# Sorted rows that carry their weight, place and batch; results scattered to token and choice; the last residual in four parts

## The chip, the cores and the metric

The kernel runs on one core of a Trainium2 chip. It is written in the Tile framework: the program names tiles and operations, the framework places the tiles, orders each engine's instructions and puts in the waits. The engines are TensorE (PE, with its weight loads shown as PEld), VectorE (DVE), ScalarE (ACT), GpSimd (POOL) and SyncE (SP). Here SP issues all plain transfers and POOL all transfers whose rows are picked by an index. Each engine takes its instructions strictly in order, so an instruction that waits holds everything behind it on that engine.

The metric is the device time of one execution in microseconds. Before the change it is 1390.96 us (median of 3 runs, 1390.5 to 1391.24).

## The reference

One block of a transformer on 2 x 1024 tokens of width 256, all in float32: attention with 16 heads of 128 (one key and value head shared by all), then a mixture of experts, 2 of 8 for each token. Both are modulated by a condition vector. Cut to what matters:

```python
h = layernorm(x) * (1 + ca) + sa
x = x + ga * attention(h)            # ends in a layernorm of its output
h = layernorm(x) * (1 + cb) + sb
x = x + gb * moe(h)

def moe(x):                          # T = 2048 tokens, H = 256, I = 176, E = 8, K = 2
    logits = x @ router_w.T
    vals, idx = top_k(logits, K)
    w = softmax(vals)
    order = argsort(idx.reshape(-1))
    xs = x[order // K]               # rows sorted by expert
    y1 = ragged_dot(xs, w1, counts)
    gate, up = split(y1, 2)
    y2 = ragged_dot(silu(gate) * up, w2, counts)
    return (y2[argsort(order)] * w[:, None]).reshape(T, K, H).sum(1)
```

`gb` is one row of 256 factors for each of the two batches.

## The kernel before

The 2048 tokens are 16 tiles of 128 rows (NT), 8 for each batch. Attention goes over them in 4 blocks of 4 tiles. In a block, for each of 16 heads and 8 key tiles, PE makes scores (L425), ACT takes the exponential (L429), PE multiplies by the values (L440) and DVE adds up the denominators (L445). Other work hangs between these steps, placed by hand through `at(h, j, f, ...)`: the queries of the next block, the settling of the block before. After the heads comes the output projection `project` (L494).

`Settle` takes a block from projection to routing. `residual` (L528 to L540) normalises the projected rows, multiplies them by `gg` and adds them to `xs`, the running activations. `norms` and `logits` (L553, L556) make the modulated, normalised rows, kept in `rows`, and multiply them by the router's matrix. `weights` picks the best two experts of a token and their shares. `count` and `bases` work out the place of each (token, choice) in a list sorted by expert, whose parts are filled up to whole tiles of 128 rows. The sums of the normalisations need `rsqrt` (L175, L176), two small operations on POOL.

There are two sorted lists (`SETS`). Set 0 holds the tokens of the first three blocks (12 tiles, 24 token and choice tiles; 31 sorted tiles with the filling). Set 1 holds those of the last block (4 tiles; 15 sorted tiles). `scatter` (L683) is an indirect DMA on POOL that writes 128 rows of `rows` to their places in `sorted_x`, a DRAM tensor that was filled with zeros earlier (L259). Set 0 is scattered while the last block's heads run, in eight groups of three; set 1 has to wait until the last block is settled.

Then the sorted tiles run, 46 of them, in a software pipeline. In step m of the loop at L922:

- `Sorted(i, m)` issues the load of 128 rows from `sorted_x` on SP (L821), into one of four buffers;
- `turn` transposes tile m on PE (L827) and copies it out of PSUM (L830 on DVE or L832 on ACT, by parity);
- `up` multiplies tile m-1 by its expert's first matrix (L845), whose place is read from a register, then silu on ACT (L853) and the product on DVE (L855);
- `turn_back` transposes tile m-3 (L861) and copies it (L864 or L866);
- `down` multiplies tile m-4 by the second matrix (L879), copies the result (L888 or L890) to `ysb`, and SP writes it to `sorted_y` (L891).

Between these stand the settling of the last block (steps 1 to 8) and, in step 9, its eight scatters. From step NM[0] + 4 = 35 on, each step also gathers for one token tile: two indirect loads on POOL (L898) fetch the rows of the two choices from `sorted_y` by `place_i`. `combine` two steps later takes the first by its share on ACT (L909), adds the second by its share on DVE (L910), multiplies by `gb` (L914), adds `xs` (L915), and SP stores the tile (L916). The gathers of set 0 can only start when all 31 sorted tiles of set 0 are in DRAM, those of set 1 when all 15 of set 1 are.

The framework orders indirect transfers that write the same tensor one after the other: their rows are only known at run time, so it can't tell that they don't overlap.

## Time and profile before

| | |
|---|---|
| median of 3 runs | 1390.96 us |
| the profiled execution, its own time | 1394.08 us |
| its span, first to last instruction | 1392.3 us |
| PE busy in the span | 1334.5 us, 96% |
| DVE, ACT, POOL busy | 681.3, 486.5, 212.2 us |
| projection of the last block ends | 1215.4 us |
| first result tile of the sorted part leaves (L891) | 1237.06 us |
| last scatter of set 1 issued (L683) | 1274.60 us |
| first gather of set 0 (L898) | 1316.67 us |
| last matmul ends | 1371.7 us |
| first gather of set 1 | 1375.46 us |
| last store issued | 1389.1 us |

Times within the profile are counted from the span's start. "Busy" is the time in which an engine worked on an instruction; PE's clock is granted by a throttle, and the profile shows it as a fraction of full speed. In the order of time each line has start and duration in us, engine, source line and operation, the tiles written and read, the shape, how many were merged, and in brackets the idle time just before and what ended it. A line of the waits has the waiting engine and line, the releaser, total us, how often, and the longest. A line of the chain of waits has start, us, and what the end of the kernel was waiting for then.

### The profile page before, as it was taken

The page shows a single profiled execution, that of the slowest core. Times are in us where ns is not written, and L with a number is a line of the kernel's source. Part 1 is how long each engine was busy: PE and PEld are TensorE (multiplying, and loading weights), DVE is VectorE, ACT ScalarE, POOL GpSimd, SP SyncE. Part 2 cuts the span into 40 slices and gives each one's busy share as a digit, 9 for nine tenths or more (in the row PEclk, how much of TensorE's full clock was granted, in tenths as well). Part 3 has the DMA queues.
Part 4 walks back from the last instruction along what each step waited for, and adds up shares of the span by engine and source line. Part 5 has one row for each costly group of instructions (what it writes and reads, how often), then busy time and mean ns, then how long its engine had stood idle before and what let it go on. Part 6 is the DMA issues. An engine that isn't in the chain of part 4 may idle for free.

```text
span 1392.3 us, 12605 instructions
## 1 busy us (share of the span) xinstructions
PE 1334.5 (96%) x4024; PEld 692.9 (50%) x4024; DVE 681.3 (49%) x1378; ACT 486.5 (35%) x947; POOL 212.2 (15%) x303
## 2 busy tenths in 40 slices
PE   7899999999999999999999999999999999989954
PEld 3444444447444444456444444474444444757733
DVE  6356665643636454545464545335474435263343
ACT  2433344441333433322333333313343333133221
POOL 4210312110100010001100000001002230002152
PEclk9999999999999999999999999999999999989977
DMA  7000000000006000010000300000000121114342
GB/s 238 1 1 31 0 31 0 31 0 31 0 0 204 1 30 0 31 31 1 0 32 0 113 0 31 1 31 0 0 31 23 53 87 46 38 57 137 111 144 91
DMA packets 44050, 58.90 MB, mean 42 GB/s; under 512 B 5008, under 2 KB 32656, under 8 KB 43984
## 3 DMA queue, kind: packets, MB, share of 16 engines
q1 hardware_dynamic: 40912, 49.70, 10.9%
q0 software_dynamic: 3072, 8.39, 2.0%
q8 instruction: 33, 0.54, 0.2%
q14 instruction: 33, 0.27, 0.1%
HBM read 39.60 MB, written 18.48 MB: 42 GB/s over the span
## 4 chain that ended last, share of the span: by engine, by line
PE 88%; DMA 4%; DVE 3%; POOL 2%; issue 2%; another core or an unknown queue 0%; ACT 0%; SPq 0%; POOLq 0%; DVEq 0%; ACTq 0%
PE s L425 30%; PE o L440 30%; PE q L388 7%; PE pr L494 7%; PE su L845 3%; PE sy L879 3%; DMA sorted_x<-hT,to 2%; PE qp L402 2%; PE den L454 1%; POOL y L898 1%; PE kv L331 1%; DMA y<-sorted_y,place_i 1%; PE ap L861 1%; PE xp L827 1%; DMA sorted_y<-ysb 1%
## 5 line engine op out<-in xcount | busy, mean ns | idle before, releaser
L425 PE MATMUL s<-qT,kT 128*128 128x512 f32 x1024 | 524.1, 594 | 0.0
L440 PE MATMUL o<-p,vs 128*128 128x512 f32 x1024 | 522.8, 593 | 1.1 <-ACT p L429 1.1
L429 ACT ACTIVATE p<-s 128x512 f32<-128x512 f32 x512 | 305.8, 597 | 502.0 <-PE s L425 491.2
L445 DVE TENSOR_TENSOR sum<-sum,p 128x512 f32<-128x512 f32 x384 | 264.3, 688 | 181.7 <-ACT p L429 177.5
L440 PEld LDWEIGHTS o<-p,vs 128*128 128x128 f32 x1024 | 193.3, 190 | 234.7 <-issue 231.5
L425 PEld LDWEIGHTS s<-qT,kT 128*128 128x128 f32 x1024 | 187.1, 190 | 205.4 <-issue 204.4
L175 POOL TENSOR_SCALAR rn_q<-rn_q 128x4 f32<-128x4 f32 x64 | 15.2, 237 | 722.4 <-DVE rn_q L291 707.3
L388 PE MATMUL q<-wq_sb,hT 128*128 128x512 f32 x256 | 121.9, 599 | 0.0
L494 PE MATMUL pr<-wout_sb,qT 128*128 128x256 f32 x512 | 113.0, 380 | 0.1
L494 PEld LDWEIGHTS pr<-wout_sb,qT 128*128 128x128 f32 x512 | 96.6, 190 | 19.3 <-issue 4.3
L445 DVE TENSOR_TENSOR sum<-p,p 128x512 f32<-128x512 f32 x64 | 44.1, 690 | 111.7 <-ACT p L429 111.5
L291 DVE TENSOR_REDUCE rn_q<-sq_q 128x4 f32<-128x512 f32 x64 | 43.7, 684 | 84.1 <-ACT sq_q L290 84.1
L176 POOL TENSOR_TENSOR rn_q<-rn_q,minus_half 128x4 f32<-128x4 f32 x64 | 82.6, 1291 | 5.3
L388 PEld LDWEIGHTS q<-wq_sb,hT 128*128 128x128 f32 x256 | 49.2, 193 | 60.6 <-issue 50.5
L845 PE MATMUL su<-w_sb,xT 128*128 x184 | 67.5, 491 | 10.6 <-ACT xT L832 5.0
L294 DVE TENSOR_TENSOR vn_q<-q,rn_q 128x512 f32<-128x512 f32 x64 | 44.2, 690 | 58.7 <-POOL rn_q L176 58.7
L290 ACT ACTIVATE sq_q<-q 128x512 f32<-128x512 f32 x64 | 38.2, 597 | 76.0 <-PE q L388 71.6
L462 DVE RECIPROCAL rden<-den 128x512 f32<-128x512 f32 x16 | 53.7, 3357 | 19.3 <-PE den L454 19.3
L470 DVE TENSOR_TENSOR qT<-qT,wide 128x512 f32<-128x512 f32 x64 | 42.3, 688 | 42.5 <-DMA wide<-spread 42.3
L879 PE MATMUL sy<-w2s,sactT 128*128 x184 | 51.4, 406 | 8.5 <-ACT y L909 5.5
L402 PEld LDWEIGHTS qp<-ident,vn_q 128*128 128x128 f32 x256 | 32.2, 143 | 37.3 <-issue 31.5
L447 ACT COPY qT<-o 128x512 f32<-128x512 f32 x64 | 37.5, 586 | 22.7 <-PE o L440 22.7
(155 smaller groups left out, 762.8 us busy)
## 6 DMA issues: line engine op xcount, KB each, us to landing
wide<-spread SPq DMA_DIRECT2D x64, 256.0 KB
x<-sorted_x SPq DMA_DIRECT2D x46, 128.0 KB
sorted_y<-ysb SPq DMA_DIRECT2D x46, 128.0 KB
sorted_x<-zero SPq DMA_DIRECT2D x1, 3968.0 KB
w_sb<-in_w_dram SPq DMA_DIRECT2D x2, 1408.0 KB
wout_sb<-in_wout_dram SPq DMA_DIRECT2D x1, 2048.0 KB
out_dram<-res SPq DMA_DIRECT2D x16, 128.0 KB
sorted_x<-zero SPq DMA_DIRECT2D x1, 1920.0 KB
```

The costliest lines, as they stand in the source:

```text
L176: nc.gpsimd.tensor_tensor(out, out, minus_half[:, : out.shape[1]], ALU.pow)
L294: nc.vector.tensor_tensor(vn, src, rn.unsqueeze(2).to_broadcast([P, n, DH]), ALU.mult)
L388: nc.tensor.matmul(q.rearrange("p h d -> p (h d)"), hT[:, self.blk * QT + i, c, :], wq_sb[:, c, ts(g, QB)], start=(c == 0), stop=(c == DC ...
L402: nc.tensor.transpose(tp[:, j, :], qn[:, j, :], ident)
L425: nc.tensor.matmul(s, kT[:, ts(b * NJ + j, P)], q.head(h), start=True, stop=True)
L429: nc.scalar.activation(p, s, AF.Exp)
L440: nc.tensor.matmul(outs[h], vs[:, b * NJ + j, :], p, start=(j == 0), stop=(j == NJ - 1))
L445: nc.vector.tensor_tensor(sums[h], first, p, ALU.add)
L462: nc.vector.reciprocal(rden, den)
L494: nc.tensor.matmul(ps, q.head(h)[:, ts(i, P)], wout_sb[:, h, :], start=(h == 0), stop=(h == HEADS - 1),)
L845: nc.tensor.matmul(u, self.xT[:, c, :], w1_flat[:, c * I2 :][:, bass.ds(at, I2)], start=(c == 0), stop=(c == DC - 1),)
L879: nc.tensor.matmul(y, self.actT[:, c, :], w2_flat[:, c * D :][:, bass.ds(at, D)], start=(c == 0), stop=(c == 1),)
```

## The change

Each sorted row grows from 256 to 260 words: the choice's weight, the row of the result that it belongs to (token x 2 + choice, an integer), and the batch. The first choice's weight is written where it is made, in `rows`; before the second choices are scattered, POOL copies the second weights and rows over the first (`choose_second`). Empty places of a sorted tile point to rows past the end, filled in with the zeros.

With that, `down` can finish a row by itself: it multiplies by the weight and by the gate of the row's batch in the one operation that takes the result out of PSUM (DVE), and an indirect DMA on POOL writes the rows to `results`, in the order of token and choice. For set 0, which holds tokens of both batches, `gates` makes the gate of each row on DVE. Reading back is then a plain load on SP of 128 x 2 x 256 words (`fetch`), and `combine` is two additions on DVE. ACT makes both PSUM copies `xT` and `sactT` of each tile now, before they went by turns to ACT and DVE.

The loads of sorted tiles are issued up to 7 steps ahead (`PRE`). The first three have buffers of their own; all others share 12 buffers (`RING`) with the fetches, and such a buffer is held until its tile's scatter has read its indices. The fetches of set 0 start in step 38.

The last block's `residual` is split: the statistics right after the projection, then one token tile in each of the steps 0 to 3; norms, logits, weights, count, bases and scatters of that block follow two to three steps later than before, with the scatters right after `bases`. All first choices of a set are scattered before all second ones.

```diff
-    hT = keep.tile([P, NT, DC, P], FP, name="hT")
-    rows = hT.rearrange("p t c q -> p t (c q)")
+    WEIGHT, TO, BATCH, ROW = D, D + 1, D + 2, D + 4
+    rows = keep.tile([P, NT, ROW], FP, name="rows")
+    hT = rows[:, :, :D].rearrange("p t (c q) -> p t c q", q=P)
...
+    for i, (t0, t1) in enumerate(SETS):
+        first_to = rows[:, t0:t1, TO].bitcast(I32)
+        nc.gpsimd.iota(
+            second_to[:, t0:t1], [[TOP * P, t1 - t0]], base=0, channel_multiplier=TOP
+        )
+        nc.vector.tensor_copy(first_to, second_to[:, t0:t1])
+        nc.vector.tensor_scalar(second_to[:, t0:t1], second_to[:, t0:t1], 1, None, ALU.add)
+    for b in range(B):
+        nc.vector.memset(rows[:, b * TPB : (b + 1) * TPB, BATCH:], float(b))
...
-    sorted_y = [dram.tile([n * P, D], FP, name=f"sorted_y{i}") for i, n in enumerate(NM)]
+    results = [
+        dram.tile([(TOP * (t1 - t0) + 1) * P, D], FP, name=f"results{i}")
+        for i, (t0, t1) in enumerate(SETS)
+    ]
...
+        def choose_second(t0, t1):
+            nc.gpsimd.tensor_copy(rows[:, t0:t1, WEIGHT], share[:, t0:t1])
+            nc.gpsimd.tensor_copy(rows[:, t0:t1, TO].bitcast(I32), second_to[:, t0:t1])
...
+        RING = 12
+        PRE = 7
+        FETCH = sum(NM) - 1 - PRE
+        def row_buffer(name):
+            return mg.tile([P, TOP * D], FP, tag="x", name=name, bufs=RING)
...
-                self.x = mx.tile([P, D], FP, tag="x", name=f"x_{self.m}")
+                if self.m < EARLY:
+                    self.x = mx.tile([P, ROW], FP, name=f"x_{self.m}")
+                else:
+                    self.x = row_buffer(f"x_{self.m}")[:, :ROW]
...
-                ysb = mg.tile([P, D], FP, tag="ysb", name=f"ysb_{m}")
-                if m % 2:
-                    nc.scalar.copy(ysb, y)
-                else:
-                    nc.vector.tensor_copy(ysb, y)
-                nc.sync.dma_start(out=sorted_y[self.i][ts(self.at, P), :], in_=ysb)
+                ysb = mg.tile([P, D], FP, tag="ysb", name=f"ysb_{m}", bufs=4)
+                nc.vector.scalar_tensor_tensor(
+                    ysb, y, self.x[:, WEIGHT : WEIGHT + 1], self.gate, ALU.mult, ALU.mult
+                )
+                nc.gpsimd.indirect_dma_start(
+                    out=results[self.i],
+                    out_offset=bass.IndirectOffsetOnAxis(
+                        ap=self.x[:, TO : TO + 1].bitcast(I32), axis=0
+                    ),
+                    in_=ysb,
+                    in_offset=None,
+                )
+            def gates(self):
+                if self.i:
+                    self.gate = gb[:, B - 1, :]
+                    return
+                self.gate = mg.tile([P, D], FP, tag="gate", name=f"gate_{self.m}")
+                nc.vector.scalar_tensor_tensor(
+                    self.gate, gb_more, self.x[:, BATCH : BATCH + 1], gb[:, 0, :],
+                    ALU.mult, ALU.add,
+                )
-        def gather(t):
...
+        def fetch(t):
+            i = 0 if t < SETS[0][1] else 1
+            at = t - SETS[i][0]
+            y = row_buffer(f"y_{t}").rearrange("p (k d) -> p k d", k=TOP)
+            nc.sync.dma_start(
+                out=y,
+                in_=results[i][TOP * at * P : TOP * (at + 1) * P, :].rearrange(
+                    "(p k) d -> p k d", k=TOP
+                ),
+            )
+            return y
+        def combine(t, y):
+            res = my.tile([P, D], FP, tag="res", name=f"res_{t}")
+            nc.vector.tensor_tensor(res, y[:, 0, :], y[:, 1, :], ALU.add)
             nc.vector.tensor_tensor(res, res, xs[:, t, :], ALU.add)
             nc.sync.dma_start(out=ot[:, t, :], in_=res)
...
-        for m in range(sum(NM) + LAG):
-            if m < NM[0]:
-                tiles[m] = Sorted(0, m)
-            elif m < len(tiles):
-                tiles[m] = Sorted(1, m - NM[0])
+        for m in range(len(which) + LAG):
+            while len(tiles) < min(m + 1 + PRE, len(which)):
+                tiles.append(Sorted(*which[len(tiles)]))
...
-            if m == 1:
-                settle.norms()
+            if m < QT:
+                settle.residual(m, m + 1)
+            elif m == QT:
+                settle.norms()
...
-            t = m - NM[0] - LAG
+            t = m - FETCH
             if 0 <= t < SETS[0][1]:
-                gathered.append((t, gather(t)))
+                fetched.append((t, fetch(t)))
```

In the changed kernel the result scatter is L935, the fetch L960, the two additions L971 and L972, the store L973, the gate L950 and the finishing of a result tile L932.

## The prediction

> **What bounds the kernel now.** I read the stretches of time first, because the page's 96% for TensorE is a mean over attention, which the change barely touches, and a last sixth, which it rewrites.
>
> ```profile
> 700.00:1000.00 300.00, 299.91 (x855) 147.69 (x854) 144.88 (x248) 106.57 (x184) 27.74 (x36) 1.00 0.07 24
> 1275.00:1300.00 25.00, 25.00 (x122) 18.74 (x121) 8.93 (x26) 7.93 (x26) 0.56 (x1) 1.00 0.35 115
> 1325.00:1350.00 25.00, 12.72 (x36) 7.82 (x34) 8.62 (x24) 4.55 (x14) 15.59 (x17) 0.71 0.51 150
> 1375.00:1393.00 18.00, 0.00 (x0) 0.00 (x0) 5.08 (x12) 2.03 (x4) 7.57 (x8) 0.54 0.29 88
> ```
>
> After the stretch come busy us of PE, PEld, DVE, ACT, POOL, then the granted clock, DMA share and GB/s. Attention is full on PE. So are the sorted tiles at 1275 to 1300, but at 1325 to 1350 PE is half idle at a clock of 0.71 while POOL is busy, and the last 18 us have no matmul at all.
>
> Next the chain of waits, for the price of one sorted tile, and the end:
>
> ```profile
> 1271.06 1.19 PE su L845 x4
> 1272.46 0.87 PE sy L879 x4
> 1273.55 1.19 PE su L845 x4
> ...
> 1372.16 2.48 DMA sorted_y<-ysb
> ...
> 1384.22 2.70 DMA y<-sorted_y,place_i
> ...
> 1388.67 0.43 DVE res L915
> ```
>
> A tile takes 1273.55 - 1271.06 = 2.49 us on PE. After the last result leaves for DRAM (1372.16) come 20.1 us of gathering and combining to the span's end at 1392.3.
>
> Third, the waits from 1300 on:
>
> ```profile
> POOL y L898 <- DMA sorted_y<-ysb: 63.1, 2, 41.1
> ACT y L909 <- DMA y<-sorted_y,place_i: 33.6, 11, 6.1
> DVE y L910 <- DMA y<-sorted_y,place_i: 14.9, 6, 8.2
> ```
>
> ACT and DVE wait inside combine for gathered rows, and what stands behind on those engines (xT, sactT, ysb) starves PE. In the order of time sy starts at 1317.09 and, six tiles later, at 1357.58: 40.5 us where 6 x 2.49 = 14.9 would do, so 25.6 us are lost there.
>
> Fourth, POOL in order of time, for a scatter that waits for the one before it, which is what the change puts into every tile:
>
> ```profile
> 1254.59 1.05 POOL L683 DMA_INDIRECT sorted_x<-hT,place_i  x1 [28.70 <-DVE sact L855]
> 1257.63 0.98 POOL L683 DMA_INDIRECT sorted_x<-hT,place_i  x1 [1.99 <-DMA sorted_x<-hT,place_i]
> 1260.34 0.96 POOL L683 DMA_INDIRECT sorted_x<-hT,place_i  x1 [1.73 <-DMA sorted_x<-hT,place_i]
> 1263.16 0.96 POOL L683 DMA_INDIRECT sorted_x<-hT,place_i  x1 [1.86 <-DMA sorted_x<-hT,place_i]
> 1266.37 0.96 POOL L683 DMA_INDIRECT sorted_x<-hT,place_i  x1 [2.25 <-DMA sorted_x<-hT,place_i]
> 1269.27 0.96 POOL L683 DMA_INDIRECT sorted_x<-hT,place_i  x1 [1.94 <-DMA sorted_x<-hT,place_i]
> 1271.93 0.96 POOL L683 DMA_INDIRECT sorted_x<-hT,place_i  x1 [1.70 <-DMA sorted_x<-hT,place_i]
> 1274.60 0.96 POOL L683 DMA_INDIRECT sorted_x<-hT,place_i  x1 [1.71 <-DMA sorted_x<-hT,place_i]
> ```
>
> From start to start 2.66 to 3.21 us, mean (1274.60 - 1254.59) / 7 = 2.86. It is over 2.49 even at its best.
>
> **The change, part by part**, on the time line of the profiled execution (span 1392.3). "R n" is the result scatter of tile n, on POOL. In the built order of the changed kernel each R waits for the landing of the one before it in the same tensor, so the 46 R form a chain.
>
> *At the start*: two integer copies, two adds and two memsets on DVE before the first z. DVE's small ones are 0.16 us each, half overlapped: +0.5 us on the path to the first transposes. The four iotas fall into POOL's idle time from 1.62 to 5.23 us; without that cover they would delay rs_p. The 24 row scatters in block 3 only change order; the two POOL copies between them, and rows of 1040 instead of 1024 bytes, lie beside a full PE. Exposed, the bytes would cost 1.6% of a 2.4 us landing.
>
> *The front of the tiles*. Before, ysb of tile 0 ends at 1236.99, since the residual, statistics and logits stand before it on DVE and two waits of PE (2.77 and 2.97 us) halve its clock. ysb_0 after: the last st_o starts at 1215.76; 0.43 + a gate of 0.47 (nearest row L910, 0.48) + mv 0.18 gives 1216.84; rsqrt to DVE 1.44 as before, 1218.28; the normalising of four tiles 2.66 as before; four adds at 0.42 for one of 1.21, 1.68; three sact 1.0; statistics 1.9; a gate, L553 and a sact 1.2: 1226.7. rsqrt 1.41, L556 0.48, ysb 0.48: 1229.1. sy_0 is ready by 1225.0 (sact_0 at 1222.0, then ap, su, ap, sy). So R0 starts at 1229.2, 7.9 us earlier than the first store. If PE's one idle stretch of 1.5 us does halve the clock, 4 us of that go. The bounds are 0 and 10.
>
> *The scatter chain*. ysb_1 stands behind 3.2 us of DVE: R1 at 1232.4. PE delivers sy_2 to sy_5 every 3.4 us (2.49 and a logits part of 0.9, as between 1238.75 and 1242.04), then every 2.49, sy_8 at 1249.8; R8 at chain pace comes at 1232.4 + 7 x 2.82 = 1252.1. The chain takes over there. For 2.82: the eight rows above had an x load and a sorted_y store beside each scatter; the stores are gone, so I go between the quiet 2.67 and the mean 2.86, nearer the latter, since a load is released by each landing. The bounds are 2.66 and 3.21, the least and the most.
>
> A sentence on the page, which the sum does not use: the Trainium skill, "DMA: Bandwidth & Descriptors", section "Anatomy of one DMA — SWDGE (gpsimd) path", gives about 2.0 us plus bytes over 436 GB/s per transfer, an estimate of 2.30 us for 128 KB, and calls descriptor generation small; by it PE and not POOL would set the pace, and the end would be that of the first rival below. The rows have 0.96 us of POOL and then 1.70 or more of landing in series, so I stay with the rows.
>
> Into this chain come the eight row scatters of the last block. place_i follows the last logits copy by 13.1 us (1241.16 to 1254.3), now from 1242.7: 1255.8. They wait for each other too, R9 to R14 stand between them, and choose_second waits for the fourth: seven steps of 2.82, 0.6 of copies and 1.0 of issue put R14 at 1277.2, where the chain alone had 1269.0. ysb has four buffers, so ysb_18 waits for R14; from there DVE, the sact behind ysb, and through it PE move at POOL's pace. R34 is at 1277.2 + 20 x 2.82 = 1333.6. SP's x loads are seven tiles ahead and lose at most four: no wait.
>
> *Reading back*. In the built order fetch y_0 takes the buffer of tile 34, so it waits for R34, though its data is complete at R30. On DVE its sum stands between ysb_35 and ysb_36. R34 lands at +2.7, the load at +5.3 (2.0 for 128 KB in the chain, 0.6 for twice the bytes), ysb_36 at +7.0, so R36 at +7.2 where the chain alone has +5.6. PE meanwhile idles some 8 us and restarts at half clock, as from 1337 to 1343 before. y_1 takes y_0's buffer, and so on: two fetches to a tile. Following SP's order, R37 is at +11.1, R38 +15.1, R39 +18.5, R40 +21.6, R41 +24.4, and four more at 2.82: R45 at +35.6 (11 x 2.82 = 31.0, so the fetches cost 4.6). R45: 1369.2. The bounds of the 4.6 are 0 and the 25.6 that the gathers lost.
>
> *The tail*. R45 lands after 2.75; four plain loads, the first 2.6 after issue; four pairs of adds at 0.8; the last store to the end 3.2, as from 1389.1 to 1392.3: 12.0 with the issue between. The bounds are 11 and 13.5. Before: 20.1.
>
> *Sum*: 1369.2 + 12.0 + 0.5 = 1381.7 against 1392.3, or -10.6. The profiled execution lies 1.3 us over the median of the runs shown (1390.96), so the forecast is **1380 us**. ACT (0.37 + 0.32 + 0.37 a tile) and DVE (0.47 + 0.33 + 0.48) are far under 2.49, so giving ACT both copies costs nothing while PE or POOL sets the pace.
>
> **Rivals.**
>
> *PE sets the pace.* If scatters come at 2.49 or faster, sy_45 is at 1249.8 + 37 x 2.49 = 1341.9, R45 at 1343.4, 5 us of fetch stall, 12.0 and 0.5: 1361, about **1360 us**. For it: the gathers leave POOL every 1.25 us. Against: no dependent scatter in the trace is under 2.66.
>
> *The chain is slower still.* 42 steps hang on the period (7 to R8, 7 row scatters, 20, and 8 not covered by fetches). At 3.21 that is 42 x 0.39 = 16.4 more: 1398, **1397 us**, slower than before. It decides from 10.6 / 42 = 0.25 more, a period of 3.07. For it: two of seven gaps are over 3.0, and a load starts with each landing. Against: twice that traffic gave 2.86.
>
> *The change doesn't do what it says*: the gathers go, but fetches that wait for buffers and stall DVE lose the same 25.6. That is 21 more, **1401 us**. Against: the fetches need no POOL, and ACT no longer waits.
>
> **How the numbers follow.** Forecast 0.61, PE's pace 0.14, slower chain 0.17, fetches 0.08. Some 0.2% (2.8 us) is about what a measurement can tell here. The forecast's own band, 1371 to 1390, is 0.22 us of period either way, cut by the other bounds; all of it is faster but for 0.02. The slower chain is half over 1395; a quarter of it is still within 0.2%. Faster 0.59 + 0.14 = 0.73; same 0.02 + 0.04 = 0.06; slower 0.21. The range 1362 to 1395 leaves out half of the first rival, half of the second and the third.
>
> **What would show it.** L935 on POOL starts near 1229, then 2.8 apart and idle on its own DMA; under 2.5 makes the first rival, over 3.07 the second. DVE's ysb waits for that DMA from tile 18 on, PE some 90% busy at a clock near 1.0 from 1280 to 1330. One idle stretch of DVE before L971, of 8 us or more, and a half clock after it. Some 12 us from the last L935 to the end. If DVE's idle time before L971 sums to over 20 us, the third rival holds. If attention ends over 1 us later than at 1215.4, my hidden edits are wrong.

## The result and the profile after

The changed kernel is slower: 1403.58 us, the median of five runs (1402.89 to 1408.93), against 1390.96. The ratio of the means is 1.0097, with a 95% interval of 1.0076 to 1.0119. The forecast was 1380 in a range of 1362 to 1395, so the sign was wrong and the time lies outside the range. The profiled execution has a span of 1401.9 us; the sum of the prediction had made it 1381.7. The case nearest to what happened is the rival "the chain is slower still", which stood at 1397; its period came true, and, as the experiments show, for another reason than the one it gave.

The stretches of time after the change, with the same columns as before (busy PE, PEld, DVE, ACT, POOL, then the granted clock):

```profile
700.00:1000.00 300.00, 300.00 (x859) 147.97 (x858) 146.63 (x251) 106.19 (x183) 27.55 (x36) 1.00 0.08 24
1275.00:1300.00 25.00, 20.52 (x94) 14.30 (x92) 7.84 (x21) 8.14 (x24) 10.16 (x10) 1.00 0.29 90
1325.00:1350.00 25.00, 18.25 (x76) 12.52 (x74) 4.12 (x11) 6.68 (x20) 7.67 (x8) 0.92 0.28 85
1375.00:1402.00 27.00, 3.23 (x16) 2.37 (x14) 5.44 (x14) 0.74 (x2) 5.32 (x6) 0.66 0.26 92
```

Between 1325 and 1350 PE went from 12.72 busy us to 18.25, as meant. But between 1275 and 1300, where it had been full, it is now busy for 20.52 of 25 us at a full clock. It has stopped setting the pace. Who sets it is seen on POOL in order of time; these are result scatters of three stretches, the middle one from the time of the fetches:

```profile
1293.30 1.19 POOL L935 DMA_INDIRECT results<-ysb,x  x1 [2.17 <-DVE ysb L932]
1296.70 1.20 POOL L935 DMA_INDIRECT results<-ysb,x  x1 [2.21 <-DVE ysb L932]
1300.07 1.20 POOL L935 DMA_INDIRECT results<-ysb,x  x1 [2.17 <-DVE ysb L932]
...
1364.51 0.96 POOL L935 DMA_INDIRECT results<-ysb,x  x1 [3.90 <-DVE res L971]
1369.41 0.96 POOL L935 DMA_INDIRECT results<-ysb,x  x1 [3.94 <-DVE res L972]
...
1387.11 0.96 POOL L935 DMA_INDIRECT results<-ysb,x  x1 [2.17 <-issue]
1390.23 0.96 POOL L935 DMA_INDIRECT results<-ysb,x  x1 [2.17 <-issue]
```

Three periods are to be read, from start to start: 3.37 us while tiles of set 0 run (1300.07 - 1296.70), 4.90 while results are read back, and 3.12 at the end, where neither a load of sorted rows nor a fetch is left. No gap between scatters to one tensor comes down to the 2.82 of the prediction. The waits from 1215 on show the queue that has formed (waiting engine and line, releaser; total us, times, longest):

```profile
POOL results L935 <- DVE ysb L932: 50.3, 24, 3.2
DVE res L971 <- DMA y<-results: 34.2, 11, 14.6
PE sy L924 <- DVE ysb L932: 14.0, 18, 2.3
```

The first line must not be read as "POOL waits for DVE". At 1296.06 a ysb starts, 0.1 to 0.2 us after the landing of the scatter issued at 1293.30 (1293.30 + 2.6, the median landing in this stretch). It is the ysb of four tiles later, which was waiting for that landing to free its buffer. It ends 0.16 us before POOL starts, so the inference picks it as the releaser. POOL's own ysb had long been there. An experiment below with 16 buffers confirms that: the period does not fall below 3.13. The order of cause is: landing, then POOL and DVE together, then PE (18 waits of sy).

The chain that ended last, at the end of the kernel (start, us, what):

```profile
1387.11 0.96 DMA results<-ysb,x
1388.06 1.94 issue
1390.01 0.22 POOLq L1064
1390.23 2.41 DMA results<-ysb,x
...
1393.55 3.90 DMA y<-results
...
1397.46 0.44 DVE res L971
```

The last scatter lands 2.41 us after its issue; the scatter before it was issued at 1387.11, landed at about 1389.52 by the same 2.41, and still the next starts only at 1390.23, 0.7 us later. Before the change, the row scatters started again much sooner: 1274.60 - 1271.93 = 2.67, and if a row scatter lands as fast, 2.67 - 2.41 leaves 0.26. That difference, and not the landing, is what the forecast had not in its sum.

The span of 1401.9 against the 1381.7 forecast, stretch by stretch (R n is the result scatter of tile n):

| stretch | forecast, us | measured, us | difference |
|---|---|---|---|
| end of attention, against before | +0.5 | +5.5 (1215.4 to 1220.88) | +5.0 |
| end of the projection to R0 | 13.8 | 13.1 (R0 at 1233.97) | -0.7 |
| R0 to R8 | 22.9 | 25.2 (1259.16) | +2.3 |
| R8 to R14 | 25.1 | 24.3 (1283.43) | -0.8 |
| R14 to R34 | 56.4 | 65.2 (1348.61) | +8.8 |
| R34 to R45 | 35.6 | 41.6 (1390.23) | +6.0 |
| R45 to the end | 12.0 | 11.7 | -0.3 |
| sum | | | +20.3 |

### The profile page after: what moved, and what is told of

Same layout as the page of the kernel before. It is cut to its first block, busy times and chain, and to the rows that moved or that the text cites. A ratio compares the mean times of both kernels' runs of the same rounds, so it can differ in the third digit from the quotient of the medians.

```text
span 1401.9 us, 12710 instructions
## 1 busy us (share of the span) xinstructions
PE 1334.3 (95%) x4024; PEld 689.3 (49%) x4024; DVE 685.4 (49%) x1383; ACT 489.7 (35%) x954; POOL 230.1 (16%) x325
## 5 line engine op out<-in xcount | busy, mean ns | idle before, releaser
L412 PE MATMUL q<-wq_sb,rows 128*128 128x512 f32 x256 | 122.1, 599 | 0.0
L412 PEld LDWEIGHTS q<-wq_sb,rows 128*128 128x128 f32 x256 | 49.2, 193 | 60.2 <-issue 50.1
L893 PE MATMUL su<-w_sb,xT 128*128 x184 | 65.2, 476 | 0.3
L935 POOL DMA_INDIRECT results<-ysb,x x46 | 47.0, 1023 | 96.3 <-DVE ysb L932 50.3
```

What stands on the lines that cost most here:

```text
L412: nc.tensor.matmul(q.rearrange("p h d -> p (h d)"), hT[:, self.blk * QT + i, c, :], wq_sb[:, c, ts(g, QB)], start=(c == 0), stop=(c == DC ...
L893: nc.tensor.matmul(u, self.xT[:, c, :], w1_flat[:, c * I2 :][:, bass.ds(at, I2)], start=(c == 0), stop=(c == DC - 1),)
L935: nc.gpsimd.indirect_dma_start(out=results[self.i], out_offset=bass.IndirectOffsetOnAxis(ap=self.x[:, TO : TO + 1].bitcast(I32), axis=0), ...
```

## The experiments

Ratios are to the kernel before, run beside each experiment, with the 95% interval. The changed kernel was measured a second time beside some of them (e10): 1405.63 us, ratio 1.0118 (1.0098 to 1.0137), with the same gaps of 3.13 and 3.37. That is the mark for what follows, beside the first 1.0097 (1.0076 to 1.0119).

> The changed kernel itself, beside the others on this chip, so that their differences can be taken on one chip. Expected: 1.009 to 1.010 of the time before, gaps of 3.13 and 3.37 as in its first profile. If the attention's end moves from 1220.9 us by over 1.5 us, part of what I took for the cost of the change there is a spread between executions.

### The words at the start (e1)

```diff
-    (iotas, copies, adds and memsets of the words before block 0)
+    empty_to = const.tile([P, len(SETS)], I32, name="empty_to")
+    def words(): ...
...
+                at(7, 1, words)
                 at(9, 0, clear_sorted)
```

> The integer words (four small iotas on POOL, two copies, two adds and two memsets on DVE) move from the start of the kernel into the second attention block; nothing else changes. Theory: their place at the start costs about 3 us, because the first softmax reciprocal on DVE began at 127.6 us in the changed kernel and at 124.3 before; then the time falls from 1403.6 to about 1400.5 and the first reciprocal starts near 124.3. Rival: they cost the 0.5 us that I had put down, and the rest is a spread between executions; then 1403 and a first reciprocal near 127.

Measured: 1401.03 us, ratio 1.0056 (1.0035 to 1.0077), span 1400.6. Two us are about what a comparison can tell, so the trace decides here. In the first 12 us, DVE of the changed kernel (start, duration):

```profile
9.13 0.51 DVE L328 SCALAR_TENSOR_TENSOR h<-xs,mv_p,one_ca 128x256 f32<-128x256 f32 x1
9.56 0.23 DVE L171 COPY rows<-second_to 128x12 int32<-128x12 int32 x2
9.77 0.48 DVE L331 SCALAR_TENSOR_TENSOR h<-h,rs_p,sa 128x256 f32<-128x256 f32 x1
10.18 0.25 DVE L172 TENSOR_SCALAR second_to<-second_to 128x12 int32<-128x12 int32 x2
```

and with the words in the second block of attention:

```profile
8.85 0.88 DVE L331 SCALAR_TENSOR_TENSOR h<-xs,mv_p,one_ca 128x256 f32<-128x256 f32 x2
9.65 0.87 DVE L334 SCALAR_TENSOR_TENSOR h<-h,rs_p,sa 128x256 f32<-128x256 f32 x2
```

The integer instructions stand between the first norms, two by two, and pull them apart. The first reciprocal of attention on DVE, a mark that every trace has, comes at 125.4 instead of 127.6 (124.3 before the change). Over all profiles of the study it is at 126.3 to 128.1, mean 127.45, in the twelve with early words and at 124.7 to 125.5, mean 125.2, in the three with late ones: 2.3 us. So the theory holds for 2.3 of its 3 us. The forecast had 0.5 for this.

The other half of the late attention is not the change's. From the first to the last reciprocal took 1064.4 us before and 1066.5 after, but profiles that share the code of that stretch gave anything from 1064.2 to 1067.5.

### Reading back: buffers, order, or the traffic itself (e2, e11, e13)

The kernel reads a tile back through buffers that it shares with the loads of sorted rows, and the first addition stands in the middle of the scatters. Own buffers for the fetches (e2):

```diff
-        RING = 12
+        RING = 16
...
-            return mg.tile([P, TOP * D], FP, tag="x", name=name, bufs=RING)
+            return mg.tile([P, ROW], FP, tag="x", name=name, bufs=RING)
...
-            y = row_buffer(f"y_{t}").rearrange("p (k d) -> p k d", k=TOP)
+            y = my.tile([P, TOP, D], FP, tag="y", name=f"y_{t}", bufs=4)
```

> The fetched results get four buffers of their own and the sorted rows a ring of 16; order and steps stay. Theory: the stretch from R36 to R40 with gaps of 3.7 to 5.2 us (22.8 us for five, where 15.7 would do) comes from fetches that share buffers with sorted tiles and hold up DVE; then these gaps return to about 3.1 and the time falls by 5 to 7 us, to some 1397. Rival: DVE waits for the fetched data in its order anyway, whoever holds the buffers; then the gaps stay over 3.7 and the time within 2 us of 1403.6.

Measured: 1405.51 us, ratio 1.0089 (1.0073 to 1.0106). The theory falls: nothing is saved. The loss moved from R36 to R40 forward to R31 to R35, where the gaps are now 6.45, 5.96, 4.11 and 4.63, and from there to the end they are 3.13 to 3.30.

Then the additions were put behind later tiles on DVE, so that no result tile has to wait for a fetched one (e11, with buffers as in e2, but six for the fetches):

```diff
-            if t >= 2 and fetched:
-                combine(*fetched.pop(0))
+            while fetched and min(36 + fetched[0][0] // 1, len(which) - 1) <= m - LAG:
+                with tc.issue_after(tiles[m - LAG].done):
+                    combine(*fetched.pop(0))
```

> As the kernel with fetch buffers of their own, six of them, but the additions of token tile t stand on DVE behind the finishing of sorted tile 36 + t, where the scheduler had put the first ones right behind tile 31. Theory, the fetch stretch loses time because DVE stands before data that is not there while result tiles wait behind it: the four long gaps (6.45, 5.96, 4.11 and 4.63 us, 8.6 more than four of 3.13) go back to 3.13, and the time falls by 7 to 9 us beside the kernel with fetch buffers alone. Rival: the transfers of the fetches slow the scatters' landing; then the gaps stay above 3.5.

Measured: 1412.47 us, ratio 1.0159 (1.0144 to 1.0175), the rival's side. POOL in order of time, in the fetch stretch:

```profile
1355.06 0.99 POOL L936 DMA_INDIRECT results<-ysb,x  x1 [3.53 <-DVE ysb L932]
1359.61 1.01 POOL L936 DMA_INDIRECT results<-ysb,x  x1 [3.55 <-DVE ysb L932]
1364.22 1.01 POOL L936 DMA_INDIRECT results<-ysb,x  x1 [3.60 <-DVE ysb L932]
```

Even with the additions out of the way the gaps are 4.5 to 4.6 us. The median from issue to landing of these scatters is 3.8 us, against 2.41 where nothing else moves. In the changed kernel the median is 3.6 between 1351 and 1375 (3.3 when it was measured again), and 2.4 on either side of it.

The opposite end: no fetch before the last scatter has landed (e13, with eight buffers for the fetches).

```diff
+            tc.add_manual_dep(getattr(got, "ins", got), sent[-1].name, SYNC, reason="last")
...
-        for t in range(*SETS[1]):
-            fetched.append((t, fetch(t)))
-        while fetched:
-            combine(*fetched.pop(0))
+        for t in range(NT):
+            combine(t, fetch(t))
```

> As the kernel with fetch buffers of its own, but no result is fetched before the last result scatter has landed; all 16 are fetched then. Theory: the scatters after tile 31 are late because the fetches' transfers lengthen their landing (median 3.6 us from issue to landing between 1351 and 1375 in the changed kernel, 2.4 elsewhere), and each longer landing is added to the series; then the gaps from R31 to R45 are all 3.13, R45 comes some 45 us after R30 (the changed kernel run again: 53.3), while the end after R45 grows from 12 to 25 or 30 us, so that the whole is slower, 1405 to 1415. Rival: the last tiles are late for another reason (the order on DVE, the loads of sorted rows); then gaps over 3.5 remain without a fetch.

Measured: 1420.43 us, ratio 1.0202 (1.0179 to 1.0225). POOL, with no fetch in flight:

```profile
1369.46 0.96 POOL L935 DMA_INDIRECT results<-ysb,x  x1 [2.18 <-DVE ysb L932]
1372.58 0.96 POOL L935 DMA_INDIRECT results<-ysb,x  x1 [2.17 <-DVE ysb L932]
```

All gaps after R31 but one (4.35) are 3.12 to 3.15. R30 to R45 takes 46.4 us, against 53.3 in e10: the fetches cost this series 7 us. Reading back afterwards costs more, since the stretch from R45 to the end is 31.4 instead of 11.7. So the fetches belong where they are; what makes them expensive is that each delays a landing for which the next scatter waits.

### What the period is made of (e4, e5, e6, e7, e14)

A result scatter reads the row numbers in x (loaded by SP), the rows in ysb (DVE), and follows the scatter before it: three releasers. A row scatter of the kernel before has its operands long since and one releaser. In e4, POOL copies the row numbers and touches ysb one tile ahead, so that both are its own work and only the landing is left to be waited for:

```diff
+                self.to = mg.tile([P, 1], I32, tag="to", name=f"to_{m}", bufs=48)
+                nc.gpsimd.tensor_copy(self.to, self.x[:, TO : TO + 1].bitcast(I32))
+                seen = mg.tile([P, 1], FP, tag="seen", name=f"seen_{m}", bufs=48)
+                nc.gpsimd.tensor_copy(seen, ysb[:, :1])
...
+            def send(self):
                 nc.gpsimd.indirect_dma_start(
```

> POOL reads one element of each result tile and copies the row numbers into a tile of its own ahead of each result scatter, so that the scatter itself waits for nothing but the scatter before it. Theory: the changed kernel's scatters are 3.13 us apart and not 2.67 to 2.86 because they have three things to wait for, held in an instruction of its own in POOL's queue (0.68 us from the landing to the next issue, against about 0.27 where a row scatter waits for one thing); then the gap falls to about 2.7 (2.95 where a gate on DVE runs beside the issue), and 35 gaps give 12 to 15 us, a time near 1390. Rival: result rows take longer to land than sorted rows; then the gaps stay at 3.1 or more and the time over 1400.

Measured: 1399.73 us, ratio 1.005 (1.0033 to 1.0066). Where one wait was left, among the first eight scatters, gaps down to 2.70 appear, for the first time in a series of results. Of the later ones many got two waits again, the second one on POOL's own work, and at the end, where nothing else moves, their gap was 3.17. The chain of waits shows what lies between a landing and the next issue there (POOLq L942 is an event-semaphore instruction, which only waits):

```profile
1366.91 2.43 DMA results<-ysb,to
1369.34 0.02 issue
1369.36 0.02 POOLq L942
1369.38 0.71 issue
1370.08 2.42 DMA results<-ysb,to
```

Two waits thus cost as much as three. In e5 one instruction does both touches, and the scatters wait for the landing alone, but for a few that also wait for something long over:

```diff
-                nc.gpsimd.tensor_copy(seen, ysb[:, :1])
+                nc.gpsimd.tensor_tensor(seen, ysb[:, :1], self.to.bitcast(FP), ALU.add)
```

> As the kernel with one wait, but POOL's touch reads the result tile and the copied row numbers together, so that no result scatter waits for POOL itself either (before, those from the ninth on had two waits and kept gaps of 3.17, while the first ones with one wait had 2.70). Theory: a second wait costs a result scatter about 0.45 us; then the gaps are 2.65 to 2.8 to the end wherever POOL is the bound, the last scatter is issued near 1375 and the time is 1386 to 1392 beside 1403.6 of the changed kernel. Rival: the late scatters were slow for another reason (fetches, DVE's order); then gaps of 3.1 remain after 1340 and the time is 1396 or more.

Measured: 1392.28 us, ratio 0.9991 (0.9981 to 1.0). The chain from 1302 and from 1362:

```profile
1302.17 2.92 DMA results<-ysb,to
1305.08 0.27 issue
1305.35 2.93 DMA results<-ysb,to
...
1362.91 2.43 DMA results<-ysb,to
1365.34 0.27 issue
1365.60 2.42 DMA results<-ysb,to
```

In the last stretch, where nothing else moves, the period is 2.69 and was 3.13 in the changed kernel: 0.44 us for the waits alone. A landing of 2.42 is followed by 0.27 us to the next start here, one of 2.41 by 0.72 in the changed kernel.

It is not the count of waits by itself, though. By the semaphores recorded in the traces, the changed kernel and the slow scatters of e4 wait for the landing in an event-semaphore instruction ahead of the issue; the issue itself waits for an engine (DVE or POOL). In e5, and in the row scatters before and after the change, the issue itself waits for the landing. Three of these have a second wait as well, held in an event-semaphore instruction and long over: two in e5 (1302.17 and 1360.21), which start 0.27 us behind the landing, and the last row scatter before the change (1274.60), with its gap of 2.67. So what costs the 0.44 is, as far as this shows, the place of the wait that ends last; no run moved that wait alone.

Between 1283 and 1324 the gaps of e5 are 3.07 to 3.21. The restart is 0.27 there too; it is the landing that takes 2.8 to 2.9 in place of 2.42. Two things are beside it, the gate on DVE and the loads of sorted rows.

The gate first, with the three waits kept (e6):

```diff
-                if self.i:
-                    self.gate = gb[:, B - 1, :]
-                    return
+                self.gate = gb[:, self.i, :]
+                return
```

> The changed kernel without the row-by-row gate on DVE for the first list: its rows are all multiplied by the first batch's gate, so the choice of the batch is left out. Theory: the issue of a scatter takes 1.20 us and not 0.96 where the gate's operation runs beside it on DVE; then all issues take 0.96 to 1.05, the gaps of 3.37 between 1286 and 1320 become 3.13, and the time falls by 2.5 to 4 us. Rival: the 0.24 us come from the loads of sorted rows in the same stretch; then 1.20 stays and the time within 1 us of 1403.

Measured: 1401.86 us, ratio 1.0055 (1.0038 to 1.0072). POOL in the stretch of set 0:

```profile
1299.16 0.96 POOL L935 DMA_INDIRECT results<-ysb,x  x1 [2.19 <-DVE ysb L932]
1302.30 0.96 POOL L935 DMA_INDIRECT results<-ysb,x  x1 [2.18 <-DVE ysb L932]
```

Every issue is 0.96 where it had been 1.20, and the gap 3.14 where it had been 3.37. In the changed kernel, DVE's gate of 0.48 us runs beside the issue:

```profile
1296.06 0.48 DVE L932 SCALAR_TENSOR_TENSOR ysb<-sy,x,gate 128x256 f32<-128x256 f32 x1 [2.15 <-PE ap L909]
1296.58 0.48 DVE L950 SCALAR_TENSOR_TENSOR gate<-gb_more,x,gb 128x256 f32<-128x256 f32 x1
```

The gate starts at 1296.58 and the issue at 1296.70: one landing has released both, POOL by way of its 0.72 us and DVE by way of a ysb. The gate adds 0.24 us to each of the ten scatters beside which it stands. The Trainium skill, "SBUF — State Buffer", section "Who interferes with whom", says that a VectorE instruction with two inputs in SBUF contends with a GpSimd instruction that reads SBUF, and calls what they share an exclusive lock. The trace agrees: gates that ended 0.24, 0.33 and 0.36 us into an issue (e12 at 1238.42; the changed kernel at 1260.42 and 1296.70) lengthened it by 0.12, 0.20 and 0.24, so each by what it ran past the first 0.12 us. A gate that ended 0.10 us into an issue (1283.43), or began 0.50 us into it (1267.89), added nothing. The gate can also be the one that becomes longer: in e5 it took 0.55 us beside the issue of 1302.17, which stayed at 1.00.

With one wait and without the gate (e14, the edits of e5 and e6 together):

> One wait for each result scatter and no row-by-row gate in the first list (its rows are all multiplied by the first batch's gate, so the choice of the batch is left out). With one wait alone the gaps were 2.69 after 1360 but 3.07 to 3.20 from 1283 to 1324, where the gate ran on DVE and each landing released a load of sorted rows. Theory: the gate on DVE makes the difference; then these gaps fall to 2.7 to 2.8. Rival: the load of sorted rows, released by the same landing, collides with the next scatter; then they stay at 3.0 or more.

Measured: 1398.32 us, ratio 1.0032 (1.0021 to 1.0042). Between 1283 and 1335 the gaps stay at 3.14 to 3.35, and at the end they are 2.69 to 2.72. The theory that the gate was what remained falls, and the landings there take 2.96 to 3.08. The rival fits, and the order of the transfers shows how. Here is the load that goes with the scatter at 1299.16 of e6, and then the one that goes with the scatter at 1302.17 of e5:

```profile
1298.48 0.32 SPq L872 DMA_DIRECT2D x<-sorted_x  x1
...
1302.53 0.32 SPq L872 DMA_DIRECT2D x<-sorted_x  x1
```

With three waits (e6) the landing frees a row buffer, SP issues the next load at once, and its bytes have moved before those of the scatter, which is issued 0.68 us later. With one wait the scatter is issued first; the row buffer is free only when DVE has written a ysb, the load comes 0.36 us behind the scatter, and both move together. The scatter then lands 0.4 to 0.7 us later. The two prices cover each other, and taking one away shows the other. No run took the loads away in this stretch, so this is read from the traces and from the end of the series, where no load is left and the landing is 2.42. R14 to R30 takes 52.1 us in e5 and in e14; e14 loses against e5 mostly before that (R0 to R14 in 51.9 us, against 48.0), which I have not taken apart.

Last, whether POOL waits for DVE at all: 16 buffers for ysb instead of four (e7).

```diff
-                ysb = mg.tile([P, D], FP, tag="ysb", name=f"ysb_{m}", bufs=4)
+                ysb = mg.tile([P, D], FP, tag="ysb", name=f"ysb_{m}", bufs=16)
```

> The changed kernel with 16 buffers in place of 4 for the result tiles. Theory, POOL's series of landings is the bound and PE and DVE only wait for it: PE runs ahead until the ring of sorted rows stops it, the waits of DVE and PE go, POOL has result tiles in store while DVE waits for the first fetch, and only the loss of the fetch stretch (about 7 us from R35 to R40) is saved: 1395 to 1398. Rival, the four buffers are themselves what slows the stage: the gaps fall to 2.5 and the time to 1375 or less. Second rival: the store runs dry and nothing is saved, 1403.

Measured: 1404.16 us, ratio 1.0079 (1.0061 to 1.0096). From R14 to R35 the gaps are 3.13 to 3.16, but for one with a lengthened issue (3.32), two late ones (4.00 and 3.91) and the one at which the series changes to the other set's tensor. The 3.37 of set 0 are gone, because DVE's ysb and gate no longer start with the landing, beside the issue; the 3.13 stay. So the ysb named as the releaser was not what POOL waited for. The whole does not gain: R0 to R45 takes 153.5 us, against 156.3 in the changed kernel, but R0 comes 2.6 us later (1236.59). In the fetch stretch the gaps are still 3.54 to 4.98, so result tiles in store did not save it.

### Taking the series apart (e3, e8, e9, e12)

If the period of a series is the cost, two series side by side should give the time back. e3 has two result tensors to each set, one for even and one for odd tiles, zeroed during attention; the fetch reads both and one more addition joins them.

```diff
+        [
+            dram.tile([(TOP * (t1 - t0) + 1) * P, D], FP, name=f"results{i}{s}")
+            for s in range(2)
+        ]
...
-                    out=results[self.i],
+                    out=results[self.i][self.m % 2],
...
+            nc.vector.tensor_tensor(y[:, 0], y[:, 0], y[:, 1], ALU.add)
```

> As the kernel with fetch buffers of its own, and each list has two result tensors, both cleared with zeros during attention; even sorted tiles scatter to one, odd ones to the other, and the reading back loads both and adds them. A scatter then waits for the one before the last. Theory, the series of landings sets the pace: result scatters come 2.49 us apart as PE delivers, DVE no longer waits for their landing, the last scatter is issued near 1348 and, with a tail of about 13 us, the span is 1361 to 1368 (the changed kernel: 1401.9). Rival, the scatters or their traffic are slow in themselves: they stay at 3.1 us or more apart and the span stays over 1395. Second rival, PE or SP becomes slower by the double fetches: scatters at 2.5, but over 15 us lost after 1335.

Measured: 1372.53 us, ratio 0.9854 (0.9837 to 0.987), with twice the bytes to read back and with the fetch buffers of e2. The stretch from 1290 to 1312:

```profile
1290.00:1312.00 22.00, 22.00 (x108) 16.52 (x107) 10.36 (x25) 8.89 (x27) 10.80 (x11) 1.00 0.47 139
```

PE is full again. The scatters come in pairs, 1.97 us apart in the mean from R20 (1290.94) to R31 (1312.62), while POOL works off what had queued up, and from R29 on every 2.49 us, PE's price of a tile. So neither the landing nor POOL's 0.96 us of issue sets the pace by itself here; waiting for one landing before the next issue does.

e8 added the late words, eight buffers for ysb and six for fetched tiles, later additions, and tiles of their own for the row numbers of set 0's row scatters:

```diff
-            to = work.tile([P, HG, DH], I32, tag="sq", name=f"to_{k}_{t}", bufs=1)[:, 0, :n]
+            to = small.tile([P, n], I32, tag="to", name=f"to_{k}_{t}")
```

> Two result tensors for each list as before, with the integer words moved into the second attention block, eight buffers for result tiles, six for fetched ones, four steps between a fetch and its additions in place of two, and row numbers of the scatters in attention in tiles of their own. The kernel with two result tensors lost about 12 us in the fetch stretch, 5 us of PE around the row scatters and 2 us at the start. Theory: most of that comes back, a span of 1354 to 1360 beside 1369.3. Rival: the fetch stretch is bound by DMA (share 0.89 there), not by DVE's order; then no more than 5 us are saved.

Measured: 1374.21 us, ratio 0.986 (0.9843 to 0.9876), a miss: no better than e3. From R0 to R45 it is 3.7 us shorter than e3 (119.5 against 123.2), as the rival had it, but attention became longer. The last edit went wrong in a way worth seeing:

```profile
1100.57 0.96 POOL L728 DMA_INDIRECT sorted_x<-rows,to  x1 [1.79 <-DMA sorted_x<-rows,to]
1101.60 0.19 POOL L197 TENSOR_SCALAR rn_q<-rn_q 128x4 f32<-128x4 f32 x1
1101.87 1.04 POOL L198 TENSOR_TENSOR rn_q<-rn_q,minus_half 128x4 f32<-128x4 f32 x1
```

The shared row-number tile had let only one group of three row scatters into POOL's queue at a time. Without it they queue up in series in front of the queries' norms rn_q, and a scatter that waits for a landing keeps all that is behind it on POOL. A transpose of PE that needs those norms waited 6.81 us at 1103.69, and attention took some 11 us longer from its first reciprocal to its last.

e9 goes back to one result tensor, and tells the scheduler that two neighbouring scatters write different rows; each then waits for the one before the last. Empty places of even and odd tiles point to two different sets of rows past the end, so that the rows do differ. It has the buffers of e2.

```diff
+                if self.at:
+                    tc.declare_no_dep(sent[self.i][-1], sent[self.i][-2], reason="other rows")
+                if self.at > 1:
+                    tc.add_manual_dep(
+                        sent[self.i][-1], sent[self.i][-3].name, SYNC, reason="the one before"
+                    )
```

> One result tensor for each list, as in the changed kernel, and fetch buffers of their own, but a result scatter waits for the one before the last in place of the last one. Their rows differ; the empty places of even and odd sorted tiles point to different rows past the end, so that two scatters in flight never write the same row. Nothing is read twice. Theory, the wait for the scatter just before is what makes the changed kernel slow: pairs of scatters 2.49 us apart in the mean, and a span of 1356 to 1366 (the kernel with fetch buffers alone: 1401.3; with two tensors, read twice: 1369.3). Rival: it was the second tensor itself that helped, two scatters in one tensor are no faster; then over 1395.

Measured: 1369.86 us, ratio 0.9855 (0.984 to 0.987), against 1.0118 for the changed kernel beside it; the span of 1367.6 is 1.6 over the expected range. It is the order of the series, then, and not the tensor or the traffic. e12 adds to it the late words, eight ysb buffers, six fetch buffers, fetches from step 36 on, and additions of tile t behind sorted tile 34 + t, as in e11:

> Scatters that wait for the one before the last, eight buffers for result tiles, the integer words in the second attention block, fetches from step 36 on and the additions of token tile t behind the finishing of sorted tile 34 + t. Theory: PE is the bound to the end at 2.49 us a tile, the last scatter is issued near 1338 to 1344 and the span is 1348 to 1356 (before: 1392.3). Rival: the fetches' own traffic or the row scatters' place still cost 8 us or more; then over 1358.

Measured: 1355.78 us (1354.45 to 1357.5), ratio 0.9756 (0.9743 to 0.9769). It beats both kernels.

```profile
1275.00:1300.00 25.00, 25.00 (x122) 18.68 (x121) 13.18 (x31) 10.29 (x31) 13.47 (x14) 1.00 0.42 125
1300.00:1325.00 25.00, 25.00 (x122) 18.76 (x121) 11.03 (x28) 10.18 (x30) 11.66 (x13) 1.00 0.69 204
```

PE is full for these 50 us. The scatters here land after a median of 3.8 us between 1313 and 1340, as late as in e11, but with two in flight the gaps are mostly 1.6 to 2.7, and PE sets the pace until 1325. The last scatter goes out at 1342.06, 48.2 us before that of the changed kernel, and 12.0 us later the kernel ends. Additions behind later tiles, a loss in e11, are part of this gain of 14 us over e9; how much each of e12's additions brought was not taken apart.

## Why the prediction was wrong, and where it was right

**The step that failed** is the price of the period: "For 2.82: the eight rows above had an x load and a sorted_y store beside each scatter; the stores are gone, so I go between the quiet 2.67 and the mean 2.86". I had asked what traffic lay beside the eight scatters, and not what each of them had to wait for, and how. Their issue itself waits for the landing; a result scatter has three releasers, and its landing is waited for in an instruction ahead of the issue. The price of that, 0.44 us in each period (e5 against the changed kernel, both at the end, where the loads and fetches are over), is in none of those rows. Of the 42 steps that the prediction put on the period, the seven row scatters did not become slower (R8 to R14 took 24.3 us for 25.1); for the other 35, 3.13 instead of 2.82 makes 35 x 0.31 = 10.9 us, which eats the 10.6 us forecast as the gain. The gate, the start and the fetches, below, make the kernel slower than before.

**The upper bound of the period** was also too low. "The bounds are 2.66 and 3.21" did not hold the 3.37 of set 0's stretch: the gate, costed only as DVE's own time, lengthens the scatter's issue from 0.96 to 1.20 (e6). In R14 to R34 (+8.8) the terms are 20 x 0.31 = 6.2 for the period, 10 x 0.24 = 2.4 for the gate, some 1.9 for two late gaps (4.66 and 3.54 instead of 3.13, from 1329.71 on), less 1.9 for the one gap of 1.26 at which the series changes to the other set's tensor. The late landing at 1329.71 has its like, a gap of 4.4 to 5.3 between 1324 and 1336, in six of the study's kernels (e1, e4, e5, e10, e11, e13); its cause was not tested.

**The start** was mis-sized: "Exposed +0.5" was right in kind and measured 2.3 (e1). The count of DVE's instructions was right; that they would be put between the first norms and hold apart pairs of them was not in the sum. By the prediction's own sign, an end over 1 us later than 1215.4, this part failed. The rest of the 5.5 us by which attention ends later is within what profiles with the same code differ by.

**The fetches** were named rightly with their mechanism: y_0 in the buffer of tile 34, one idle stretch of DVE before the first L971, R34 + 5.3 for the landing. It came at R34 + 5.17 (1353.78), after an idle stretch of 11.64 us. The term was mis-sized: 4.6 forecast, 41.6 - 11 x 3.13 = 7.2 measured, because the traffic of the fetches lengthens the landing from 2.41 to 3.6, which the prediction had not priced; e13 gives 6.9 for the same thing.

**Right** were the front of the tiles (13.1 for 13.8), the tail (11.7 for 12.0), the copies on ACT, which cost nothing (PE is full beside them in e3 and e12), and the chain as the new bound.

**The rivals.** "The chain is slower still" named its point of decision, a period of 3.07, and the period was 3.13: it ended on the slower side as worked out. Its reason, a load that starts with each landing, was not the cause: with three waits the loads cost the scatters nothing (3.14 beside them in e6, 3.13 at the end without them). Its 1397 was 6.6 us short. It had 0.17, and the sentence against it, "twice that traffic gave 2.86", rested on the same wrong question. "PE sets the pace", 1360 us, lies between e9 (1369.86) and e12 (1355.78, with further edits), in which the series was broken, so the value of that case was sized about right; its condition was not met by the change. "Fetches lose the same 25.6" was wrong: they lose 7. That its 1401 lies nearest to the measured time is luck. Its sign, over 20 us of idle DVE before L971, came true all the same (34.2 us, of which 19.1 in the fetch stretch and 15.0 in the tail): idle time of DVE did not measure the loss, since the series set the pace.

The sentence from the Trainium skill, "DMA: Bandwidth & Descriptors", section "Anatomy of one DMA — SWDGE (gpsimd) path", gave 2.30 us as an estimate for one transfer. The landing measured 2.41, close to it. The 0.27 to 0.72 us from there to the next issue come on top, and so PE with its 2.49 did not set the pace.

**Where the gain went.** The gathers' 25.6 us of starved PE and 8.4 us of the tail (20.1 to 11.7) are indeed gone. They were given back by the series: PE would need 2.49 us for a tile, and a scatter goes out only every 3.13 to 3.37.

## What to carry to other kernels

Before a step is put into a loop, ask whether it waits for its own previous completion. If so, its pace is the landing plus the restart, and a single duration in a trace says nothing of it; take the row of an operation that *waits for the same things in the same way*, not just one of the same size and traffic. And where writes to one tensor go to different rows, saying so to the scheduler, so that two are in flight, can be worth more than all of the rest: it took the changed kernel from a ratio of 1.0118 (1.0098 to 1.0137) to 0.9855 (0.984 to 0.987), with fetch buffers that alone gave nothing.

## What the runs showed of the hardware

- A DMA issue on POOL started 0.27 us after the landing that it waited for itself (e5, with landings of 2.42 and of 2.9), and 0.72 to 0.75 us after it where the landing was waited for in an event-semaphore instruction ahead of the issue, with three waits (changed kernel) or two (e4): periods of 2.69, 3.13 and 3.17. In the changed kernel each of these scatters has such an instruction of its own on POOL's queue, with a median of 2.65 us.
- An instruction of DVE with two tensors in SBUF that was under way when the issue of an indirect DMA began lengthened that issue by what it ran past its first 0.12 us: 0.24 us in the ten scatters beside a gate. A ysb, whose first tensor is in PSUM, ran beside the issue at 1377.69 (1377.58 to 1378.06) and left it at 0.96.
- An indirect DMA of 128 KB landed after 2.41 us with nothing beside it, after 2.8 to 3.1 where a load of sorted rows was issued 0.4 us behind it (e5, e14), and after 3.3 to 3.8 (medians) while fetches of 256 KB and stores of 128 KB were in flight.
- The releaser that a trace infers can be a second effect of the same event: ysb was named 24 times as what POOL waited for, and with four times as many buffers for it the period was still 3.13.
